# Second-layer queries: a product split in two levels, a key bias sum moved to ScalarE, and where the work around them stands

## The chip, the cores and the metric

The kernel runs on one NeuronCore of a Trainium2 chip. The metric is the device time of one execution in microseconds (us), lower is better. In what follows TensorE is PE in the profile, VectorE is DVE, ScalarE is ACT, GpSimd is POOL, and SyncE, which only issues loads and stores here, is SP.

## The reference

Two cross-attention layers are applied to x (8 batches of 100 rows and 1024 columns), each against the same context (8 x 1444 x 512), all in float32:

```
layer 0:  Q = x Wq + bq, K = ctx Wk + bk, V = ctx Wv + bv
          x <- x + (softmax over keys(Q K^T / 32) V) Wo + bo
layer 1:  q = x Wq + bq, k = ctx Wk + bk, v = ctx Wv + bv
          w = softmax over the QUERIES (axis 1) of q k^T / 32
          x <- layernorm(w v + x) * gamma + beta
```

The output is x. In layer 1 the softmax runs over the 100 query rows of one batch, for each of the 1444 keys.

## The kernel before, in words

**Algebra.** Scores are not made from keys. The kernel first multiplies the two weight matrices of a layer, Wq Wk^T (a product called qk, 1024 x 512), and uses x (Wq Wk^T) as queries of width 512, called g0T and g1T, against the raw context. In the same way Wv Wo of layer 0 becomes one matrix, vo. What the biases add to the scores is a vector for each batch, the key bias (`c`), made from `kb`, the sum over the 8 chunks of x of chunk times a column of weights.

**Strassen-like products.** Most products are made with seven half-size products for eight (`weight_products`, `queries`, `project0`, `project1`); a line like `left_sums` makes the four sums S1 to S4 of the left operand, T1 to T4 are those of the right. The seven results are called x, z, y, x, w, x, y by the PSUM bank that they go to, and VectorE adds them to their blocks. `inner_product` does the same once more inside one of the seven, with names like g_z_x, vo_w_y, o_q_x: the z, w or q product of the outer seven, in seven again. Seven with 1/8 less work each level, for extra sums on VectorE. In `queries(1, ...)`, the queries of layer 1, the products z (4 matmuls become 7 of half the width, and so on) and w are split a second time; the last one, y with S4 and B22, is not.

**Order.** The order of PE is the program's own. The steps are generators (`yield`, `next`, `run`, `islice`) that are advanced by hand, so that the matmuls of two stages alternate. The order of the other engines is a scheduler's, except where `vector.in_order` or `keep_in_program_order` pins an instruction. [...]

**Stages in time** (of the profiled execution): qk of layer 0 (4 to 52 us), vo (52 to 100), queries of layer 0 (100 to 137), qk of layer 1 (137 to 184), attention of layer 0, where the scores of batch b + 2 (`s`, line 923) alternate with the weighted context rows of batch b (`A`, line 894) (184 to 351), the projection `project0` (o_..., to 381), the queries of layer 1 (g_..., 381 to 413), attention of layer 1 (413 to 605, with `project1` and the finishing of rows between) and the last batch.

**The places that the change touches.**

- Line 107: eight matmuls on a tile of ones at the start, while the first weights load. A matmul in float32 stands as two records in the trace.
- `weight_products` for vo0 (lines 490 to 510): VectorE makes T2, then the second half of a scaled sum (`accs[...][1]()`, four operations of 1024 columns on a prob tile), adds the two z banks, and makes S2 in place of S1 (tile vo_s). The product `product(X, S2, T2, False)` follows, named vo_x.
- `project0`, its last part: W is the inner w product (o_w_x, o_w_z, o_w_y, ...) whose first step is run, then the o_x banks are added to x (`add(1, 0, 1, X_)`), then the rest of W is run.
- `queries`: S4 is made in the place of A12, after g_y. Steps that `yield` let the caller put other work between.
- `key_bias_sums("kb1", ...)`: eight VectorE operations (one `tensor_scalar`, seven `scalar_tensor_tensor` of 800 columns, tile kb) spread over the steps of the queries. Layer 0's kb0 is already made in another way, by `scaled_sum`: ScalarE scales each chunk into a tile of its own, and transfers that add (`transfer_added`, on POOL's queue, line 567) sum them in pairs.
- The first scores of layer 1, `scores(0)` (16 matmuls s of 361 columns), then the last step of the queries (product y, g_y), then the scores of batch 1. The key bias c is made two matmuls before the end of the scores of batch 0 and read by ScalarE, which moves the scores to the tile prob. Then VectorE makes 16 transposes (w<-prob), three maxima (negmax), ScalarE the exponentials, VectorE the reciprocal and the product that ends w. PE's first A matmul of batch 0 reads w.
- `LATER` tells for (layer, batch) how many steps of that softmax are made at once with the scores; the others are left to the caller. The softmax of batch 0 is not in it, so all of it is put out right after the scores and ahead of g_y's adds.
- Buffers: `unit` is a pool of 10 (weights, context rows c, transposed context cT, rooms of sums); `bank` a pool of 6 PSUM banks and `bank2` one of 2; `row` and `weight_rows` pools of 3.

Of the kernel before, what the change touches and what calls it, by code (L numbers as in the profile page):

```python
# [27 lines left out]
ALU = mybir.AluOpType  # L28
# [4 lines left out]
B, T, E = 8, 100, 1024  # L33
# [13 lines left out]
G = 4  # L47
GT = G * T
SETS = (range(0, 4), range(4, 7), range(7, 8))
LATER = {(1, 5): 0, (1, 7): 16}  # L50
SCALE = 1.0 / math.sqrt(E)
EPS = 1e-6

# [2 lines left out]
def two_layer_cross_attention(ctx: ExitStack, tc: tile.TileContext, a: dict, out: bass.AP):  # L56
# [11 lines left out]
    def bank(name):  # L68
        return psum.tile([P, 512], F32, tag="ps", name=name)

    def bank2(name):
        return psum2.tile([P, 512], F32, tag="ps2", name=name)
# [31 lines left out]
    ones = const.tile([P, P], F32, tag="ones", name="ones")  # L104
    nc.vector.memset(ones, 1.0)
    warm = bank("warm")
    for _ in range(8):
        nc.tensor.matmul(warm[:, :P], ones, ones, start=True, stop=True)
    ident = const.tile([P, P], F32, tag="ident", name="ident")
    make_identity(nc, ident)  # L110
# [29 lines left out]
    def run(*parts):  # L140

        parts = list(parts)
        while parts:
            parts = [g for g in parts if next(g, parts) is not parts]
# [35 lines left out]
    def combine(to, x, y, op, engine=vector):  # L180
        for t, p, q in zip(to, x, y):
            engine.tensor_tensor(t, p, q, op)
# [69 lines left out]
        add(0, 1, Y)  # L252
        yield

    def inner_product(name, lhs, rhs, nb, width, t, put, add, right=None, left=None, ahead=False, spare=bank2):

        h, w = nb // 2, width // 2
        m = len(singles(lhs)) // 2

        def quarters(x, n):
            if len(x) == 1:
                return ([x[0][:, m * k : m * k + m, c]] for c in halves(n) for k in range(2))
            return ([x[m * k + i][:, c] for i in range(m)] for c in halves(n) for k in range(2))

        def room(x, t):
            t = t.rearrange("p (i n) -> p i n", i=m)  # L270
            return [t] if len(x) == 1 else [t[:, i, :] for i in range(m)]

        A11, A12, A21, A22 = quarters(lhs, nb * P)
        B11, B21, B12, B22 = quarters(rhs, width)
        lw, rw = m * h * P, 0 if right else m * w
        S1, T1 = room(lhs, t[:, :lw]), right or room(rhs, t[:, lw : lw + rw])

        S2, S3, S4, T2, T3, T4 = A11, A21, A12, B11, B12, B21
        if ahead:

            S2, S4 = (room(lhs, t[:, o : o + lw]) for o in (lw + rw, 2 * lw + rw))
            if not right:
                T2, T4 = (room(rhs, t[:, o : o + rw]) for o in (3 * lw + rw, 3 * lw + 2 * rw))
        if right:
            T1, T2, T3, T4 = right

        if left:
            S1, S2, S3, S4 = left

        def second():  # L290
            combine(T2, B22, T1, ALU.subtract)
            combine(S2, S1, A11, ALU.subtract)

        def fourth():
            combine(T4, B21, T2, ALU.subtract)
            combine(S4, A12, S2, ALU.subtract)

        combine(S1, A21, A22, ALU.add)
        combine(T1, B12, B11, ALU.subtract)
        combine(S3, A11, A21, ALU.subtract)  # L300
        combine(T3, B22, B12, ALU.subtract)
        if ahead:
            second()
            fourth()

        def product(ps, left, right, fresh):
            half_product([ps], left, right, fresh, h, w)

        def steps():
            X = bank(f"{name}_x")  # L310
            product(X, A11, B11, True)
            put(0, 0, X)
            if not ahead:
                second()
            yield
            Z = spare(f"{name}_z")
            product(Z, A12, B21, True)
            add(0, 0, Z)
            if not ahead:
                fourth()  # L320
            yield
            Y = bank(f"{name}_y")
            product(Y, S1, T1, True)
            put(1, 1, Y)
            yield
            product(X, S2, T2, False)
            put(0, 1, X)
            yield
            W = spare(f"{name}_w")
            product(W, A22, T4, True)  # L330
            put(1, 0, W)
            yield
            product(Y, S4, B22, False)
            add(0, 1, Y)
            yield
            product(X, S3, T3, False)
            add(1, 1, X)
            add(1, 0, X)
            yield

        return steps()
# [5 lines left out]
    def weight_products(name, left, right, l_width, r_width, scaled, between=None):  # L347
# [91 lines left out]
        def add(r, c, banks):  # L439
            for j in range(2):  # L440
                to = block(r, c, j)
                vector.tensor_tensor(to, to, banks[j].rearrange("p (n w) -> p n w", n=per), ALU.add)
# [53 lines left out]
        if name != "qk0":  # L496
            T2, T4 = B11, B21
            combine(T2, B22, T1, ALU.subtract)
            if name == "vo0":
                accs[scaled[0][0]][1]()  # L500
            add(0, 0, Z)
        combine(S1, S1, A11, ALU.subtract)
        S2 = S1
        if name != "vo0":
            combine(A21, A11, A21, ALU.subtract)
        if name != "qk0":
# [146 lines left out]
    def queries(layer, w, u, between=None):  # L653
# [17 lines left out]
        def add(r, g, banks):  # L671
            for j in range(2):
                to = dst[g][:, 2 * r + j, :]
                vector.tensor_tensor(to, to, banks[j][:, :GT], ALU.add)
# [13 lines left out]
            return put, add  # L688

        def pair(n):  # L690

            return [(bank2 if layer and n == "y" else bank)(f"g{layer}_{n}{j}") for j in range(2)]

        def product(banks, lhs, rhs, fresh):
            half_product(banks, lhs, rhs, fresh, nb, GT)
# [1 line left out]
        t = None  # L697

        def inner(n, lhs, rhs, put, add, right=None, at=0, left=None):
            spare = bank if layer else bank2  # L700
            return inner_product(f"g{layer}_{n}", lhs, rhs, nb, GT, t[:, at:], put, add, right, left, spare=spare)

        def four(t):

# [2 lines left out]
        def steps():  # L707
            nonlocal t
            S3, S4 = A21, A12
            if layer:  # L710
                combine(S1, A21, A22, ALU.add)
                yield
                combine(S2, S1, A11, ALU.subtract)
                yield
                combine(S3, A11, A21, ALU.subtract)
                yield
            T1, T2 = ([wide(f"g{layer}_t{n}")] for n in (1, 2))
            if layer:
# [29 lines left out]
            if layer:  # L748

                vector.in_order = False  # L750
                yield
                vector.in_order = True
                S4 = A11
                combine(S4, A12, S2, ALU.subtract)
                _, more = parts(0, 0)
                Z = inner("z", A12, B21, more, more, four(T3[0]))
                combine(T2, B22, T1, ALU.subtract)
                run(Z)
                combine(T3, B22, B12, ALU.subtract)
            else:  # L760
                combine(S4, A12, S2, ALU.subtract)
# [7 lines left out]
            V = half_steps(X, S3, T3, False, nb, GT)  # L769
            for n, _ in enumerate(inner("w", A22, T1, *parts(1, 0))):  # L770
                next(V)
                if layer:
                    yield
                if layer == 0 and n == 1:
                    between()
                elif layer == 0 and n == 3:

                    add(0, 1, Y)
                    _, more = parts(0, 1)
                    Q = inner("q", S4, B22, more, more, four(T2[0]), E)  # L780
            if layer == 0:
                next(Q)
                run(V)
                yield
                run(islice(Q, 4))
                add(1, 0, X)
                add(1, 1, X)
                run(Q)
                vector.in_order = False
            else:  # L790
                run(V)
                add(1, 0, X)
                add(1, 1, X)
                vector.in_order = False
                yield
                product(Y, S4, B22, False)
                add(0, 1, Y)
            yield

        return dst, steps()  # L800
# [212 lines left out]
    def project0(AS, A0):  # L1013
# [10 lines left out]
        def pair(n, bank=bank):  # L1024
            return [bank(f"o0_{n}{j}") for j in range(2)]
# [4 lines left out]
        def add(j, r, g, banks):  # L1030
            e = 4 * j + 2 * r
            add_to_queries([e, e + 1], g * GT, GT, banks)
# [22 lines left out]
        product(X_, A_[0], B11, True)  # L1055
        combine(T2, B22, T1, ALU.subtract)
        add(1, 0, 0, X_)
        Y = pair("y")
        product(Y, S[0], T1, True)
        combine(T4, B21, T2, ALU.subtract)  # L1060
# [18 lines left out]
        add(1, 1, 1, Y)  # L1079
        product(X_, S_[1], T2, False)  # L1080

        next(W)
        add(1, 0, 1, X_)
        run(W)
        add(1, 0, 1, Y)
# [212 lines left out]
            vector.in_order = False  # L1298
    next(o0)
    next(queries1)  # L1300
    run(o0)

    kb1, more = key_bias_sums("kb1", wqbk1)
    steps = queries1
    for n, _ in enumerate(islice(steps, 5 + 7)):
        if n > 2:
            vector.in_order = True
            next(more, None)
    run(more)
    biases1 = key_biases("c1", kb1, bqbk1)  # L1310
    next(biases1)
    vector.in_order = False
# [12 lines left out]
    run(islice(scores1, LC * NB - 2))  # L1325
    key_bias[1] = next(biases1)
    run(scores1)
    run(steps)
    run(first_scores(1, 1, softmax1))

    finished = {(4, 2): 0, (4, 16): 1, (4, 30): 2, (5, 34): 3, (7, 2): 4, (7, 15): 5, (7, 28): 6}
# [43 lines left out]
```

## Time and profile before

| | us |
|---|---|
| median of 3 runs | 635.04 (634.66 to 635.53) |
| the profiled execution's own time | 634.84 |
| its span, first to last instruction | 632.9 |
| PE busy | 621.5 |
| DVE busy | 487.1 |
| ACT busy | 163.9 |
| POOL busy | 102.2 |
| DMA, mean rate | 218 GB/s |

The profile is one execution. A row of a timeline gives the start, the time from the first to the last of the records merged in it, the engine, the line, the operation, what is written and read, the shape, and in brackets the idle time before it and what ended that. A row of the waits gives the total, the number and the longest. Matmuls are pipelined: the ends shown for PE are modelled and reach past the next start, so the step from start to start is the better measure of a product.

### The profile page before, as it was taken

The numbers are of one execution on the slowest core, as the hardware profiler recorded it, in microseconds if no ns is written. First come the engines' busy times: TensorE is split into PE (matmuls) and PEld (weight loads), VectorE is DVE, ScalarE is ACT, GpSimd is POOL, SyncE is SP. The second block draws the span as 40 slices with busy tenths as digits, with TensorE's granted clock in tenths as the row PEclk, the third lists the DMA queues.
The fourth block names the chain that finished last, engine by engine and source line by source line (L and its number), as shares of the span: only waits on it lengthen the run. The fifth ranks groups of instructions, "written<-read, shape, count | busy, mean of one in ns | idle before, by whom it ended". The sixth has DMA issues, their size and how long they took to land.

```text
span 632.9 us, 10570 instructions
## 1 busy us (share of the span) xinstructions
PE 621.5 (98%) x4142; PEld 534.2 (84%) x4142; DVE 487.1 (77%) x995; ACT 163.9 (26%) x380; POOL 102.2 (16%) x133
## 2 busy tenths in 40 slices
PE   9999999999999999999999999999999999999994
PEld 8886467688985999999989666756999999999992
DVE  2987979996885797666758687968777659898886
ACT  1322012324304234423230001113433240325301
POOL 2110101112230000000000001008111220544054
PEclk9999999999999999999999999999999999999998
DMA  8969848335999788988942308255888990599002
GB/s 272 293 136 348 274 140 272 68 81 111 203 315 382 283 311 299 327 307 306 312 155 88 101 0 325 96 194 192 295 305 307 316 324 2 201 330 332 27 22 84
DMA packets 52521, 138.27 MB, mean 218 GB/s; under 512 B 4403, under 2 KB 8755, under 8 KB 52471
## 3 DMA queue, kind: packets, MB, share of 16 engines
q1 hardware_dynamic: 46792, 120.85, 55.1%
q0 software_dynamic: 5280, 16.26, 11.7%
q8 instruction: 33, 0.54, 0.3%
q10 hardware_dynamic: 398, 0.47, 0.2%
q14 instruction: 18, 0.14, 0.1%
HBM read 123.36 MB, written 3.28 MB: 200 GB/s over the span
## 4 chain that ended last, share of the span: by engine, by line
PE 90%; DMA 3%; DVE 3%; issue 1%; POOL 1%; ACT 0%; POOLq 0%; DVEq 0%; SPq 0%
PE s L923 25%; PE A L894 25%; PE qk_x L163 6%; PE o_x L163 5%; PE g_x L163 4%; DMA vo<-in_L_xattn_Wo 3%; PE o_y L163 3%; PE g_y L163 3%; PE vo_x L163 2%; PE qk_y L163 2%; PE qk_z L163 2%; DVE vo L96 1%; PE o_z L163 1%; PE o_w L163 1%; PE qk_w L163 1%
## 5 line engine op out<-in xcount | busy, mean ns | idle before, releaser
L894 PE MATMUL A<-w,c 120*128 120x100 f32 (+1 forms) x1536 | 249.6, 265 | 0.0
L894 PEld LDWEIGHTS A<-w,c 120*128 120x128 f32 (+1 forms) x1536 | 218.0, 190 | 2.8
L96 DVE STREAM_TRANSPOSE w<-prob 32x384 f32<-32x384 f32 (+1 forms) x256 | 143.7, 561 | 27.6 <-ACT prob L962 9.7
L923 PE MATMUL s<-cT,g1T 128*100 128x131 f32 (+2 forms) x592 | 122.8, 296 | 0.0
L923 PE MATMUL s<-cT,g0T 128*100 128x131 f32 (+2 forms) x592 | 122.7, 296 | 0.0
L923 PEld LDWEIGHTS s<-cT,g1T 128*100 128x100 f32 x592 | 78.4, 167 | 8.6 <-issue 0.3
L923 PEld LDWEIGHTS s<-cT,g0T 128*100 128x100 f32 x592 | 78.2, 167 | 8.4 <-PE c L593 0.4
L935 ACT ACTIVATE prob<-s,c 100x393 f32<-100x393 f32 (+2 forms) x64 | 34.5, 560 | 112.7 <-PE s L923 99.5
L1111 ACT ACTIVATE w<-w,negmax 120x100 f32<-120x100 f32 (+1 forms) x96 | 34.8, 364 | 82.7 <-DVE negmax L96 82.7
L955 DVE TENSOR_REDUCE maxima<-prob 100x1 f32<-100x394 f32 (+3 forms) x32 | 16.5, 528 | 23.4 <-ACT prob L935 23.1
L1321 POOL DMA_DIRECT2D wv<-in_L_xattn_Wv x1 | 0.8, 772 | 191.2 <-PE o_x L163 191.2
L163 PE MATMUL qk_x<-qk 128*128 128x256 f32 x128 | 29.7, 380 | 0.0
L1130 POOL TENSOR_TENSOR part<-w 120x500 f32<-120x500 f32 x8 | 10.9, 1368 | 112.9 <-DVE rstd L1205 28.6
L163 PEld LDWEIGHTS qk_x<-qk 128*128 128x128 f32 x128 | 23.3, 190 | 3.0 <-ACT qk L437 0.2
L669 ACT ACTIVATE g1T<-g_x,k 128x400 f32<-128x400 f32 x4 | 2.4, 594 | 69.2 <-PE g_x L163 69.0
L1111 ACT ACTIVATION_READ_ACCUMULATOR w<-w,negmax 120x1 f32 (+1 forms) x96 | 17.9, 187 | 0.0
L1210 POOL TENSOR_TENSOR z<-z,vectors 100x1024 f32<-100x1024 f32 x7 | 16.5, 2356 | 8.2 <-ACT z L1209 8.2
L96 DVE TENSOR_TENSOR xT<-xT,o_x 128x400 f32<-128x400 f32 (+1 forms) x32 | 15.8, 539 | 2.2 <-PE o_x L163 2.0
L1188 PE MATMUL z<-ident,xT 128*100 128x128 f32 x64 | 16.3, 273 | 0.0
L1209 ACT ACTIVATE z<-z,rstd 100x1024 f32<-100x1024 f32 x7 | 8.0, 1149 | 31.9 <-POOL rstd L1206 31.9
L1192 DVE SCALAR_TENSOR_TENSOR z<-vectors,r,z 100x512 f32<-100x512 f32 x16 | 11.8, 740 | 4.8 <-PE z L1188 4.8
L163 PE MATMUL vo_x<-vo 128*128 128x512 f32 x32 | 15.3, 595 | 0.0
(415 smaller groups left out, 987.8 us busy)
## 6 DMA issues: line engine op xcount, KB each, us to landing
cT<-in_ctxT SPq DMA_DIRECT2D x64, 722.0 KB, 6.3
c<-in_ctx SPq DMA_DIRECT2D x48, 768.0 KB, 8.3
c<-in_ctx SPq DMA_DIRECT2D x16, 512.0 KB, 5.9
vo<-in_L_xattn_Wo SPq DMA_DIRECT2D x8, 512.0 KB, 10.1
qk<-in_L_xattn_WqT SPq DMA_DIRECT2D x8, 512.0 KB
qk<-in_L_xattn_WqT SPq DMA_DIRECT2D x15, 256.0 KB, 5.8
c<-in_ctx SPq DMA_DIRECT2D x16, 224.0 KB, 5.9
xT<-in_xT SPq DMA_DIRECT2D x2, 1600.0 KB
```

The costliest lines, as they stand in the source:

```text
L96: ins = getattr(nc.vector, op)(*args, **kw)
L163: nc.tensor.matmul(banks[n // per][:, n % per * width : (n % per + 1) * width], lhs[i][:, n * P : (n + 1) * P], rhs[i], start=(fresh and i ...
L894: nc.tensor.matmul(ps[:, k * T : (k + 1) * T], c[m // CQ][:r, m % CQ, k * P : (k + 1) * P], w[:r, m, :], start=(m == 0 and k == 0), stop=( ...
L923: nc.tensor.matmul(banks[n // per][:T, cuts[n] - o : cuts[n + 1] - o], q[:, k, t0 : t0 + T], cT[k][:, cuts[n] : cuts[n + 1]], start=(k == ...
L935: nc.scalar.activation(p[:, part], ps[:T, : part.stop - part.start], AF.Identity, bias=key_bias[layer][:T, b : b + 1], scale=SCALE,)
L955: nc.vector.tensor_reduce(maxima[:, n : n + 1], p[:, part], AX.X, ALU.max)
L1111: nc.scalar.activation(w[:r, m0 + m, :], w[:r, m0 + m, :], AF.Exp, bias=negmax[:r, m : m + 1], accum_out=total[:r, m : m + 1])
L1130: add(part, w[:MR, 0:5, :], w[:MR, 5:10, :], ALU.add)
L1188: nc.tensor.transpose(ps[:T, e * P : (e + 1) * P], xT[:, 4 * j + e, b * T : (b + 1) * T], ident)
L1192: nc.vector.scalar_tensor_tensor(z[:, half], bv1[j][:T], s["r"], ps[:T, :], ALU.mult, ALU.add)
L1209: nc.scalar.activation(z, z, AF.Copy, scale=rstd)
L1210: nc.gpsimd.tensor_tensor(z, z, beta[:T], ALU.add)
```

## The change

Seven edits; the last three are small moves:

1. The last product of layer 1's queries (y with S4 and B22) is made by `inner_product` (q), seven products of 200 columns for eight matmuls of 400. It stands at the same place of PE's order, after the scores of batch 0. The banks that the inner z and w products use change to make room for it (the `spare` argument goes; y goes to `bank`).
2. S4 of layer 1's queries gets a buffer of its own (one more `unit`) and is made before the first product; `project0` gets one more `yield`, so that this step comes between its parts.
3. `kb1` is made like kb0: ScalarE scales seven chunks into seven tiles, six adding transfers sum them, a seventh adds the sum to VectorE's one chunk.
4. The softmax of batch 0 (`LATER[(1, 0)] = 0`) is put out along the steps of the split product: three transposes after each of its last three yields, the rest behind it.
5. Six matmuls for eight at the start.
6. In vo0, S2 is made before the second half of the scaled sum and the adding of z.
7. In `project0`, four steps of W for one are run before the o_x banks are added.

Stores, outputs and all other products stay. In PE's order nothing else changes. On DVE the sequence between the key bias and the first maximum of batch 0 becomes: the add of q_x, T2, S2, the add of q_z, T4, S4, the adds of q_y and q_x, 3 transposes, the add of q_w, 3 transposes, the add of q_y, 3 transposes, two adds of q_x, 7 transposes. On ACT one of the four prob<-s moves of batch 1 comes to stand ahead of the exponentials of batch 0. On POOL's queue the seven adding transfers stand among the loads of wv, gamma, beta and bv: three, wv, gamma, one, beta, bv, one, bv, two.

```
-LATER = {(1, 5): 0, (1, 7): 16}
+LATER = {(1, 0): 0, (1, 5): 0, (1, 7): 16}
...
-    for _ in range(8):
+    for _ in range(6):
         nc.tensor.matmul(warm[:, :P], ones, ones, start=True, stop=True)
...
             combine(T2, B22, T1, ALU.subtract)
-            if name == "vo0":
-                accs[scaled[0][0]][1]()
-            add(0, 0, Z)
+            if name != "vo0":
+                add(0, 0, Z)
         combine(S1, S1, A11, ALU.subtract)
         S2 = S1
+        if name == "vo0":
+            accs[scaled[0][0]][1]()
+            add(0, 0, Z)
...
         def pair(n):
-            return [(bank2 if layer and n == "y" else bank)(f"g{layer}_{n}{j}") for j in range(2)]
+            return [bank(f"g{layer}_{n}{j}") for j in range(2)]
...
                 combine(S3, A11, A21, ALU.subtract)
+                yield
+            if layer:
+                S4 = [unit(f"g{layer}_s4")[:, :E].rearrange("p (c l) -> p c l", c=H)]
+                combine(S4, A12, S2, ALU.subtract)
                 yield
...
-                S4 = A11
-                combine(S4, A12, S2, ALU.subtract)
...
             for n, _ in enumerate(inner("w", A22, T1, *parts(1, 0))):
                 next(V)
-                if layer:
-                    yield
                 if layer == 0 and n == 1:
                     between()
-                elif layer == 0 and n == 3:
+                elif n == 3:
                     add(0, 1, Y)
                     _, more = parts(0, 1)
                     Q = inner("q", S4, B22, more, more, four(T2[0]), E)
...
                 vector.in_order = False
                 yield
-                product(Y, S4, B22, False)
-                add(0, 1, Y)
+                vector.in_order = True
+                for _ in Q:
+                    yield
+            vector.in_order = False
...
         add(1, 0, 0, X_)
+        yield
         Y = pair("y")
...
-        next(W)
+        run(islice(W, 4))
         add(1, 0, 1, X_)
         run(W)
...
     next(o0)
     next(queries1)
+    next(o0)
+    next(queries1)
     run(o0)
-    kb1, more = key_bias_sums("kb1", wqbk1)
+    tiles = [t[:, : B * T] for t in prob] + [weight_rows(f"kb1_{n}")[:, : B * T] for n in range(3)]
+    kb1, more = key_bias_sums("kb1", wqbk1, tiles + [row("kb1_6")[:, : B * T]])
+    run(more)
     steps = queries1
-    for n, _ in enumerate(islice(steps, 5 + 7)):
-        if n > 2:
-            vector.in_order = True
-            next(more, None)
-    run(more)
+    run(islice(steps, 5))
+    vector.in_order = True
     biases1 = key_biases("c1", kb1, bqbk1)
...
     key_bias[1] = next(biases1)
     run(scores1)
-    run(steps)
+    softmax = batches[0]["softmax"]
+    for n, _ in enumerate(steps):
+        run(islice(softmax, 3 if n > 2 else 0))
+    run(softmax)
     run(first_scores(1, 1, softmax1))
```

More of the change, by code (lines that the diff above doesn't have):

```diff
@@ L253, in seven_products, with inner_product @@
         yield
-    def inner_product(name, lhs, rhs, nb, width, t, put, add, right=None, left=None, ahead=False, spare=bank2):
+    def inner_product(name, lhs, rhs, nb, width, t, put, add, right=None, left=None, ahead=False):
         h, w = nb // 2, width // 2
@@ L315, in steps @@
             yield
-            Z = spare(f"{name}_z")
+            Z = bank2(f"{name}_z")
             product(Z, A12, B21, True)
@@ L328, in steps @@
             yield
-            W = spare(f"{name}_w")
+            W = bank2(f"{name}_w")
             product(W, A22, T4, True)
@@ L699, in inner @@
         def inner(n, lhs, rhs, put, add, right=None, at=0, left=None):
-            spare = bank if layer else bank2
-            return inner_product(f"g{layer}_{n}", lhs, rhs, nb, GT, t[:, at:], put, add, right, left, spare=spare)
+            return inner_product(f"g{layer}_{n}", lhs, rhs, nb, GT, t[:, at:], put, add, right, left)
         def four(t):
@@ L788, in steps @@
                 run(Q)
-                vector.in_order = False
             else:
```

## The prediction

> **What bounds the kernel now.** I read the page's busy times first, then the waits of TensorE (PE), then the timeline of each engine around the places that the change touches.
>
> ```profile
> PE 621.5 (98%) x4142; PEld 534.2 (84%) x4142; DVE 487.1 (77%) x995; ACT 163.9 (26%) x380; POOL 102.2 (16%) x133
> ```
>
> PE is busy 98% of 632.9 us, so a gain can only be PE work taken out or one of PE's few idle gaps closed. The waits of PE name all of those gaps but the tail:
>
> ```profile
> PE warm L108 <- DVE ones L105: 1.1, 1, 1.1
> PE vo_x L163 <- DVE vo_s L96: 1.0, 1, 1.0
> PE o_w_y L163 <- DVE xT L96: 0.6, 1, 0.6
> PE g_z_x L163 <- DVE g_t L96: 0.4, 1, 0.4
> ```
>
> The change aims at the second and third and at the matmuls of the last query product. Around that product there is a place with little room, in the timelines of PE, VectorE (DVE) and ScalarE (ACT):
>
> ```profile
> 422.61 5.54 PE L163 MATMUL g_y<-xT,qk 128*128 128x400 f32 x16
> 427.98 9.89 PE L923 MATMUL s<-cT,g1T 128*100 128x361 f32 x32
> 437.71 0.36 PE L894 MATMUL A<-w,c 120*128 120x100 f32 x2
> ```
> ```profile
> 421.99 0.23 DVE L650 TENSOR_SCALAR c<-c,bqbk 128x8 f32<-128x8 f32 x1
> 424.26 9.46 DVE L96 STREAM_TRANSPOSE w<-prob 32x384 f32<-32x384 f32 x16 [2.05 <-ACT prob L935]
> 433.75 0.57 DVE L96 TENSOR_TENSOR g1T<-g1T,g_y 128x400 f32<-128x400 f32 x1
> 434.24 1.51 DVE L96 TENSOR_REDUCE negmax<-w 120x4 f32<-120x400 f32 x3
> ...
> 436.63 0.66 DVE L96 TENSOR_TENSOR w<-w,rtotal 120x400 f32<-120x400 f32 x1
> ```
>
> PE needs the first group of softmax weights w of batch 0 at 437.71; DVE delivers it at 436.63 + 0.66 = 437.29. No wait of PE shows, but the margin is 0.4 us, and DVE is packed from 424.26 on: 16 transposes at 0.59, an add, the maximum at 434.24, then 3.05 us through ACT's exponentials to w.
>
> [...]the 16 warm records take 3.50 us (0.219 each for 128 columns), the next 8, of 256 columns, take 1.89 us: the same time for twice the columns. [...]what the change puts ahead of the transposes delays them in full. The trace shows the strictness: at 373.73 two o_x adds stand ahead of a finished o_w_z.
>
> **The change part by part**, in the clock of this profile.
>
> *Warm-up, 8 to 6 matmuls* (16 to 12 records). They end at 1.06 + 12 x 0.21 = 3.6 instead of 4.4. The first loads were issued at 0.74 and land 3.2 us later at the earliest, 3.9; so qk_x starts near 3.95 instead of 4.40, part of it still at half clock: **-0.36**. At most -0.45[...]. Nothing takes it back: the four chunks of T4 end between 15.8 and 19.1 and qk_w uses one every 1.73 from 18.2; most loads of vo wait for PE's own releases; and the last Wo lands at 63.4, 0.9 ahead of its use by vo_z at 64.3.
>
> *vo: S2 ahead of the scaled sum.*
>
> ```profile
> 66.13 7.03 PE L163 MATMUL vo_y<-vo_s 128*128 128x512 f32 x16
> 74.20 7.10 PE L163 MATMUL vo_x<-vo,vo_s 128*128 128x512 f32 x16 [1.04 <-DVE vo_s L96]
> ```
>
> vo_x waits for vo_s, made at 73.63 behind four sums of 1024 columns (67.82 to 72.5) and two vo_z adds (72.44 to 73.7). After the change the four vo_s (1.43) come at 67.8 and end at 69.3; vo_y ends at 73.1 and vo_x follows at once: **-1.1** (idle 1.04 plus start-up). The sums and adds then end where vo_s ended, and T4 keeps its time of 77.4 against a need at 80.1. On to 98 DVE has 2.2 and 1.0 us idle, so it follows. Both ends: -1.0 to -1.2.
>
> *o0: four steps of W ahead of the two o_x adds.* The second o_w_y waits at 374.7 for the first one's add, which stands behind two o_x adds of 0.5. In the new order w_x, w_z, w_y, w_x are added by 374.8 and that wait goes. Late next: the o_x adds end at 375.85 and the third o_x product wants its second bank at 375.67, 0.2 lost. o_x began at 376.15; seven products at 0.336 from 372.91 end at 375.3: 0.8 less 0.2 = **-0.6** (0.3 to 0.8).
>
> *S4 made sooner*, in a buffer of its own. One DVE operation (1.22) moves from 386.9 to 355.1, ahead of T4 and T3 of project0. T4 ends at 357.3 for o_w at 359.48, T3 at 358.2 for o_x at 362.16, and DVE's idle 0.91 and 1.44 there take it up: **0**. Without those gaps, +1.2 at most. At 386.9 DVE was waiting for PE anyway: no gain there. The buffer comes from the stream pool: loads of batch 2 (one c block, one cT block) now wait for the split product, until about 425 and 427.5, instead of 420 and 422.8. With 6 to 8 us to landing they come by 436, for use after 442: **0**.
>
> *Key bias sum.* DVE loses seven of eight operations (0.63 + 7 x 0.96, about 6.7), but PE waited for none of them: **0** directly. ACT gains seven of about 1 us; it is idle from before 386, and four can run from 373, when xT's first half is final. The other three end at about 387, delaying g1T<-g_x from 386.2 to 387, needed at 397. On POOL's queue seven adding transfers of 400 KB interleave with wv, gamma, beta and bv. In the trace such a transfer took 4.0 to 4.8 alone, wv and the vectors 11 to 13 together. First three 375 to 385; kb_1<-kb_2 behind wv until about 391; then three in a row at 4.8: about 406. VectorE reads it at 415: room of 9 us, **0**. wv slips by about 3 us to 393 and is not used before its sums on POOL, which now start when PE leaves qk at 412.
>
> *The last product.* Out: 16 records g_y, 5.37. In: 7 products of 4 records of 200 columns, 0.675 each, 4.73. Its closest row is g_z, the same seven in a row on the same engines: 392.06 to 397.20 is 5.14, since its fourth product waits for DVE's S2. I take 5.14: **-0.23** of PE; ends 0 and -0.64. s then ends at 437.5.
>
> *What stands ahead of the transposes.* The eight VectorE operations that the split product puts there (add, T2, S2, add, T4, S4, add, add) have g_z's rows as their pattern:
>
> ```profile
> 393.01 0.36 DVE L96 TENSOR_TENSOR g1T<-g1T,g_z_x 128x200 f32<-128x200 f32 x1 [1.52 <-PE g_z_x L163]
> 393.29 0.57 DVE L96 TENSOR_TENSOR g_t<-xT,g_t 128x400 f32<-128x400 f32 x1
> 393.78 0.42 DVE L96 TENSOR_TENSOR qk<-g_t,qk 128x256 f32<-128x256 f32 x1
> ...
> 395.21 0.35 DVE L96 TENSOR_TENSOR g1T<-g1T,g_z_y 128x200 f32<-128x200 f32 x1
> 395.48 0.35 DVE L96 TENSOR_TENSOR g1T<-g1T,g_z_x 128x200 f32<-128x200 f32 x1
> ```
>
> The first add comes 0.95 after the product's start (392.06); the last starts at 395.48 and frees DVE 0.28 later, 3.7 after the start. From 422.6 that is 426.3. The transposes start at 426.3 instead of 424.26. Between them are put q_w, q_y and two q_x adds (4 x 0.28), and one g_y add (0.49) goes from ahead of the maximum. The maximum starts at 426.3 + 9.46 + 1.12 = 436.9 instead of 434.24; + 3.05 gives w at 440.0. ACT puts one prob<-s of batch 1 ahead of the exponentials, done by 436.3, so no later. PE is ready at 437.5 and waits 2.5: A begins at 440.0 instead of 437.71: **+2.3** (1.7 to 2.8), with the -0.23 in it. Behind the waiting matmul all of PE queues. Nothing takes this back: A of batch 1 has its w at 453.6 for 457.5 and both move together.
>
> *Sum*: -0.36 - 1.1 - 0.6 + 2.3 = **+0.25**. On the profiled execution's own 634.84 (span 632.9 and 1.9 around it) that is 635.1; its time lies 0.2 below the median 635.04, so 635.3.
>
> **Rivals.**
>
> *No wait at A.* If the split product's VectorE work found room in the 2.05 us that DVE is idle at 422.2, w would come as before and all gains stay: 635.04 - 2.06 - 0.23 = **632.8**. For it: that idle time exists. Against: the operations end 2 us after it, since each waits for a product of 0.675, and four adds come later.
>
> *The key bias is late* (slower; times in this profile's clock, in which all of the stage moves together). PE's c product at 421.4 needs two DVE operations of 1.2 after the last adding transfer. It decides from a landing at about 418.9. If POOL's last four transfers take 9 us each (as beside wv) instead of 4.8, from 387 they land at 423: 4 us of wait ahead of everything counted, **639.4**. Against: only wv and the vectors run beside them, and those land by 394.
>
> [...]
>
> *The split saves nothing*: with two levels PE has 14 x 200 columns for 8 x 400, an eighth less; as g_z shows, waits can eat it. That is in the forecast already: DVE ends last, not PE.
>
> **How the numbers follow.** About 0.2% (1.27 us) is what a measurement of this kernel can tell from no change. Forecast (gains of about 2 against a wait of about 2.3): 0.68, own range 634.3 to 636.3 (each part at its ends, some up and some down). No wait at A or a much shorter one: 0.15. Late bias 0.05, slow window 0.06, another wait of over 1 us that I don't see 0.06: 0.17. So faster 0.15, same 0.68, slower 0.17, and the likeliest case is no change. Leaving out some 0.1 on each side, the range is 634.0 to 636.8.
>
> **What would show it.** Right: PE's waits lose vo_x and o_w_y and gain one of about 2.5 at A <- DVE w between 437 and 440; DVE's first maximum of batch 0 14.3 after the last product starts (11.6 before); qk_x from about 3.95; c without a wait. Wrong: no wait at A, or c waiting for c_sums, or the first 8 us at half clock.

## The result, and the profile after

| | before | after |
|---|---|---|
| median | 635.34 (634.66 to 637.44, 5 runs) | 637.83 (637.67 to 638.36, 5 runs) |
| profiled execution, own time | 634.84 | 637.67 |
| its span | 632.9 | 635.9 |
| PE busy | 621.5 | 622.2 |

The ratio is 1.0046, with a 95% interval of 1.0034 to 1.0059: slower by 2.5 us by these medians, by some 2.9 by the ratio, where no change (635.3) was forecast. All times are in microseconds.

Read the waits of PE first. Of the changed kernel (total, number, longest):

```profile
PE A L895 <- ACT w L1113: 2.7, 1, 2.7
PE vo_q_x L163 <- DVE vo L96: 1.1, 1, 1.1
PE warm L108 <- DVE ones L105: 1.1, 1, 1.1
PE g_z_x L163 <- DVE g_t L96: 0.3, 1, 0.3
PE vo_w_x L163 <- DVE vo L96: 0.2, 1, 0.2
```

The waits of vo_x and o_w_y are gone, and the one at A has come, all as forecast. But vo_q_x and vo_w_x are new, and no step of the prediction has them.

The timeline of DVE around S2 of vo (the changed kernel) tells where they come from:

```profile
68.45 0.43 DVE L96 TENSOR_TENSOR vo_s<-vo_s,vo 128x256 f32<-128x256 f32 x1 [1.09 <-PE vo_y L163]
70.17 0.43 DVE L96 TENSOR_TENSOR vo_s<-vo_s,vo 128x256 f32<-128x256 f32 x1 [1.29 <-PE vo_y L163]
71.89 0.43 DVE L96 TENSOR_TENSOR vo_s<-vo_s,vo 128x256 f32<-128x256 f32 x1 [1.29 <-PE vo_y L163]
73.60 0.43 DVE L96 TENSOR_TENSOR vo_s<-vo_s,vo 128x256 f32<-128x256 f32 x1 [1.29 <-PE vo_y L163]
73.95 0.75 DVE L96 TENSOR_SCALAR prob<-vo,L_xattn_bv 128x1024 f32<-128x1024 f32 x1
...
79.77 2.49 DVE L96 TENSOR_TENSOR vo<-vo,vo 128x512 f32<-128x512 f32 x4
```

S2 is written over S1 (`combine(S1, S1, A11, ...)`, tile vo_s), and vo_y, running from 66.54, still reads S1. Each of the four operations waits for vo_y to leave its chunk, 1.72 apart. DVE stands idle for 1.09 + 3 x 1.29 = 4.96 with the scaled sum queued behind it. In the old order that sum filled just this time (the kernel before):

```profile
67.82 0.74 DVE L96 TENSOR_SCALAR prob<-vo,L_xattn_bv 128x1024 f32<-128x1024 f32 x1
68.60 3.92 DVE L96 SCALAR_TENSOR_TENSOR prob<-vo,L_xattn_bv,prob 128x1024 f32<-128x1024 f32 x3
...
73.63 1.43 DVE L96 TENSOR_TENSOR vo_s<-vo_s,vo 128x256 f32<-128x256 f32 x4
```

In the changed kernel T4 ends at 79.77 + 2.49 = 82.3, where the prediction kept 77.4.

The PE timeline of the changed kernel then shows both sides, the gain and what it costs:

```profile
66.54 7.03 PE L163 MATMUL vo_y<-vo_s 128*128 128x512 f32 x16
73.40 7.03 PE L163 MATMUL vo_x<-vo,vo_s 128*128 128x512 f32 x16
80.60 1.21 PE L163 MATMUL vo_w_x<-vo 128*128 128x256 f32 x4 [0.16 <-DVE vo L96]
...
97.57 1.13 PE L163 MATMUL vo_q_x<-vo 128*128 128x256 f32 x4 [1.13 <-DVE vo L96]
```

vo_x follows vo_y 6.86 later, as forecast (8.07 before). But vo_w_x needs T4, and DVE stays late up to the vo_q sums: from vo_w_x to the first g_x PE takes 20.88 instead of 19.09. The whole stretch from vo_z to g_x takes 101.48 - 59.67 = 41.81 instead of 40.96.

The place of the split product, first PE with the waiting A, then DVE:

```profile
423.04 0.84 PE L163 MATMUL g_q_x<-xT,g_s 128*128 128x200 f32 x4
...
428.11 9.90 PE L924 MATMUL s<-cT,g1T 128*100 128x361 f32 x32
440.72 0.43 PE L895 MATMUL A<-w,c 120*128 120x100 f32 x2 [2.71 <-ACT w L1113]
```
```profile
422.42 0.83 DVE L652 TENSOR_SCALAR c<-c,bqbk 128x8 f32<-128x8 f32 x1
423.92 0.36 DVE L96 TENSOR_TENSOR g1T<-g1T,g_q_x 128x200 f32<-128x200 f32 x1 [0.67 <-PE g_q_x L163]
...
426.39 0.35 DVE L96 TENSOR_TENSOR g1T<-g1T,g_q_x 128x200 f32<-128x200 f32 x1
426.77 1.74 DVE L96 STREAM_TRANSPOSE w<-prob 32x384 f32<-32x384 f32 x3
...
437.59 1.52 DVE L96 TENSOR_REDUCE negmax<-w 120x4 f32<-120x400 f32 x3
...
440.05 0.58 DVE L96 TENSOR_TENSOR w<-w,rtotal 120x400 f32<-120x400 f32 x1
```

The product takes 428.11 - 423.04 = 5.07 (before 5.37). The eight operations (add, T2, S2, add, T4, S4, add, add) occupy DVE until 426.7, the first maximum comes 14.55 after the product's start (before 11.63), and w is done at 440.6. A begins 17.68 after the product's start, against 15.10. The waits list names ACT for it, which is writing the next group of w at that moment. But A begins 0.09 after the end of DVE's product (440.63), and in d and g below 0.11 and 0.10 after it, so the wait is for DVE, as forecast; the time was lost ahead of that product, by the late transposes.

The span's 3.0 is put together from marks on PE (starts of products) in the two profiles:

| stretch | before | after | difference | forecast |
|---|---|---|---|---|
| start to vo_z | 59.27 | 59.67 | +0.40 | -0.36 |
| vo_z to g_x | 40.96 | 41.81 | +0.85 | -1.1 |
| o_w_x to o_q_x | 5.93 | 5.29 | -0.64 | -0.6 |
| last product of queries to A | 15.10 | 17.68 | +2.58 | +2.3 |
| all the rest | | | -0.2 | 0 |

### The profile page after: what moved, and what is told of

It reads as the page before. It is cut to its first block, busy times and chain, and to the rows that moved or that the text cites. A ratio compares the mean times of both kernels' runs of the same rounds, so it can differ in the third digit from the quotient of the medians.

```text
span 635.9 us, 10627 instructions
## 1 busy us (share of the span) xinstructions
PE 622.2 (98%) x4150; PEld 535.4 (84%) x4150; DVE 485.7 (76%) x1004; ACT 170.2 (27%) x387; POOL 108.1 (17%) x140
## 4 chain that ended last, share of the span: by engine, by line
PE 90%; DVE 7%; issue 1%; POOL 1%; ACT 0%; POOLq 0%; DVEq 0%; ACTq 0%
PE A L895 24%; PE s L924 24%; PE qk_x L163 7%; PE o_x L163 5%; PE g_x L163 4%; DVE vo L96 3%; PE o_y L163 3%; PE qk_z L163 2%; PE qk_y L163 2%; PE g_y L163 2%; PE o_z L163 1%; PE o_w L163 1%; PE vo_x L163 1%; PE qk_w L163 1%; PE vo_y L163 1%
## 5 line engine op out<-in xcount | busy, mean ns | idle before, releaser
L569 POOL DMA_DIRECT2D prob<-prob x8 | 6.9, 856 | 209.3 <-PE o_y L163 184.5
L960 ACT ACTIVATE prob<-prob,negmax 100x1444 f32<-100x1444 f32 x8 | 12.0, 1498 | 11.2 <-DVE negmax L958 11.2
```

The lines of the kernel that those rows point to most:

```text
L960: nc.scalar.activation(p, p, AF.Exp, bias=negmax, accum_out=total)
```

## The experiments

Two groups of four kernels; those of a group ran on one chip beside the kernel before (medians 635.08 in the first group, 634.95 in the second). Each ratio is to that. PE marks of all of them:

| kernel | ratio, interval | median | clock full at | vo_z | vo_z to g_x | product to A |
|---|---|---|---|---|---|---|
| a_warm8 | 1.0057 [1.0036, 1.0077] | 639.25 | 4.60 | 59.49 | 41.80 | 17.67 |
| b_vo_back | 1.0046 [1.0032, 1.0061] | 638.24 | 6.71 | 60.34 | 39.69 | 17.68 |
| c_s2_elsewhere | 1.0032 [1.0021, 1.0044] | 637.22 | 6.74 | 60.27 | 39.69 | 17.68 |
| d_no_split | 1.0010 [1.0000, 1.0019] | 635.59 | 5.41 | 59.68 | 41.79 | 15.34 |
| e_three_moves | 0.9968 [0.9956, 0.9979] | 633.28 | 6.61 | 60.26 | 39.69 | 15.10 |
| f_two_moves | 0.9972 [0.9960, 0.9984] | 633.56 | 6.61 | 60.48 | 39.69 | 15.10 |
| h_nosplit_s2 | 0.9983 [0.9973, 0.9993] | 633.99 | 4.27 | 59.52 | 39.70 | 15.34 |
| g_split_room | 0.9984 [0.9977, 0.9992] | 634.00 | 6.15 | 59.98 | 39.69 | 15.36 |

"Clock full at" is when the trace of the profiled execution has PE's clock turn from half to full: 4.13 before, 5.52 after. In the profile after, the qk_x records (256 columns each) follow one another at 0.43 ahead of it and at 0.22 behind it; in the one before, the warm records (128 columns) at 0.21 and 0.11. This is called the turn below; a drop is a later return to half clock, which the tables of stretches show as a granted clock of 0.50.

**a_warm8.** The theory under test: six warm-up matmuls make the clock turn late.

```
-    for _ in range(6):
+    for _ in range(8):
         nc.tensor.matmul(warm[:, :P], ones, ones, start=True, stop=True)
```

> The changed kernel (637.8) with eight warm-up matmuls again. Theory (the shorter warm-up with its 0.3 us gap lets the clock turn full one step later: 5.52 us for 4.13): the turn comes back to about 4.1 us, the mean clock to 0.997, and the time falls by 0.8 to 637.0. Rival (the turn comes at a random phase, whatever the warm-up): mean clock between 0.995 and 0.997 from run to run, median within 0.3 of 637.8.

639.25: slower, not faster. The turn at 4.60 did come earlier than in the profile after, and vo_z only 0.18 earlier, so this kernel alone doesn't decide the theory; e and f below do. Something else shows, in the table of stretches of this kernel (time, then busy time and number of instructions of PE, PEld, DVE, ACT, POOL, then the granted clock, DMA share, GB/s):

```profile
434.70:438.10 3.40, 3.11 (x11) 1.41 (x9) 3.29 (x7) 0.62 (x2) 0.00 (x0) 1.00 0.90 259
438.10:441.51 3.41, 0.99 (x9) 1.02 (x10) 1.96 (x6) 3.41 (x19) 0.00 (x0) 1.00 1.03 336
441.51:444.92 3.41, 3.41 (x19) 3.41 (x19) 2.13 (x5) 2.32 (x9) 1.47 (x3) 0.50 0.11 46
444.92:448.30 3.38, 3.38 (x34) 3.38 (x33) 3.25 (x7) 0.00 (x0) 2.13 (x5) 1.00 0.12 8
```

The wait at A lies almost wholly within one 3.41 stretch, PE is busy 0.99 of it, and the next stretch runs at half clock: 19 matmul records in it, 34 in the one after. At half the rate that should cost an estimated 3.41 / 2 = 1.7 on top of the wait, and it does: from A to the end this profile takes 196.87, the profile after 195.18. Three of the five executions (639.25 to 639.65) have a mean clock of 0.994, the other two (638.20 and 638.27) of 0.995 and 0.996, which fits a drop in three of them. In the profile after, no drop follows the same wait. Stretches of the same length, laid out from its own turn at 5.52, divide the wait in two, with PE busy 2.45 and 1.66:

```profile
435.56:438.97 3.41, 2.45 (x9) 1.02 (x7) 3.32 (x7) 1.29 (x5) 0.00 (x0) 1.00 0.90 292
438.97:442.38 3.41, 1.66 (x15) 1.69 (x16) 1.65 (x5) 3.41 (x21) 0.00 (x0) 1.00 0.86 265
442.38:445.80 3.42, 3.42 (x35) 3.42 (x34) 2.42 (x5) 1.65 (x5) 2.07 (x4) 1.00 0.05 19
```

**b_vo_back.** The changed kernel with vo in the old order:

```
             combine(T2, B22, T1, ALU.subtract)
-            if name != "vo0":
-                add(0, 0, Z)
+            if name == "vo0":
+                accs[scaled[0][0]][1]()
+            add(0, 0, Z)
         combine(S1, S1, A11, ALU.subtract)
         S2 = S1
-        if name == "vo0":
-            accs[scaled[0][0]][1]()
-            add(0, 0, Z)
```

> The changed kernel with the order of before in vo0 (sums and z adds ahead of S2). Theory (S2 written over S1 has to wait for vo_y, chunk by chunk, so DVE stands idle 5 us and T4 ends at 82 for 77.4): the waits vo_w_x and vo_q_x go, vo_x <- vo_s of 1.0 comes back, PE loses 0.7 less between vo_z and the queries of layer 0: 637.1. Rival (the loss there comes from loads that fell otherwise): the wait at vo_q_x stays at 1 us and the time at 637.8.

The new waits in vo are gone: 39.69 from vo_z to g_x, 2.12 less than after. The time did not follow (638.24). In the profile the late turn (6.71) takes 0.67 back at vo_z, and the drop behind the wait at A, at 440.20 to 443.62, takes 1.58 more. Of the other executions only the mean clock is known (0.991 to 0.996). The wait of 1.0 at vo_x, which was expected to return, did not:

```profile
67.20 7.03 PE L163 MATMUL vo_y<-vo_s 128*128 128x512 f32 x16
74.07 7.03 PE L163 MATMUL vo_x<-vo,vo_s 128*128 128x512 f32 x16
```
```profile
73.33 1.42 DVE L96 TENSOR_TENSOR vo_s<-vo_s,vo 128x256 f32<-128x256 f32 x4
```

This says something about the kernel before. PE came 1.07 later to vo_z, but S2 came no later (73.33, before 73.63): ahead of it DVE waits for loads of WvT and Wo in both profiles, until 60.20 and 63.16 here, 60.49 and 63.46 before. So the wait of 1.04 in the profile before is what an early PE finds; when PE is late, S2 is there already.

**c_s2_elsewhere.** The new order, but S2 gets the place of A11, which vo_y doesn't read:

```
-        combine(S1, S1, A11, ALU.subtract)
-        S2 = S1
+        S2 = A11 if name == "vo0" else S1
+        combine(S2, S1, A11, ALU.subtract)
```

> The changed kernel with S2 of vo0 written over A11, which PE has read long before, for over S1. Theory (the write over an operand in use is the whole trouble): DVE makes S2 at once near 67.5, no DVE idle before it, vo_x follows vo_y, T4 ends near 77, the waits vo_w_x and vo_q_x go: 1.8 less than 637.8, 636.0, and 1.1 less than the kernel with the order of before there. Rival (the sums behind it are late anyway): only the 0.7 comes back, 637.1.

637.22, ratio 1.0032. The waits of PE in this kernel:

```profile
PE A L895 <- ACT w L1113: 2.7, 1, 2.7
PE warm L108 <- DVE ones L105: 1.1, 1, 1.1
PE g_z_x L163 <- DVE g_t L96: 0.4, 1, 0.4
```

Neither vo_x nor vo_w_x nor vo_q_x waits. So it was the place of S2 that made the new order lose. That the new order gains over the old one isn't shown here: b, with nearly the same turn, takes the same 39.69, and the two intervals overlap (medians 638.24 and 637.22). This profile too has one stretch at half clock behind the wait at A (440.23 to 443.64, after a stretch with PE busy 0.92 of 3.41), which is why it gains less in time than in vo and misses the 636.0 expected.

**d_no_split.** The changed kernel with the last product whole, the banks as before, and the softmax of batch 0 at once:

```
-LATER = {(1, 0): 0, (1, 5): 0, (1, 7): 16}
+LATER = {(1, 5): 0, (1, 7): 16}
...
-                vector.in_order = True
-                for _ in Q:
-                    yield
+                product(Y, S4, B22, False)
+                add(0, 1, Y)
...
```

> The changed kernel with the last query product whole again and the softmax of batch 0 put out at once; S4 early, key bias by ScalarE and the three small moves stay. Theory (VectorE's work of the split product ahead of and among the transposes is what A waits for): no wait of PE at the first A of layer 1; from the start of the last product to that A 15.1 us for 17.7: 2.6 less, 635.2. Rival (the key bias by ScalarE and transfers makes c or prob late): a wait at A or c of over 1 us stays and the time is above 636.5.

635.59, 2.2 below the changed kernel's median: the split and its order on DVE cost 17.68 - 15.34 = 2.34 in the trace. No wait at A is left, but A stands 0.24 later than before, and DVE and POOL tell why:

```profile
422.46 0.83 DVE L652 TENSOR_SCALAR c<-c,bqbk 128x8 f32<-128x8 f32 x1
```
```profile
420.78 2.48 POOL L182 TENSOR_TENSOR wv_s<-wv,wv_s 128x512 f32<-128x512 f32 x2
```

The operation on c took 0.23 before and takes 0.83 here. With S4 made sooner the buffer of qk comes free at the last g_x, so that POOL's sums of wv begin at 413 (428 before) and run beside it. It is 0.83 in after, c and d, in which they do, and in h; it is 0.23 in before, e and g, in which they come later. In after, c and d it ends 0.02 to 0.03 after the last of these sums (423.29 and 423.26 here). What makes it 0.60 longer beside them was not shown: no run here took POOL's sums alone away.

**e_three_moves.** The kernel before with only the three small moves, S2 written over A11:

```
-    for _ in range(8):
+    for _ in range(6):
...
-            if name == "vo0":
-                accs[scaled[0][0]][1]()
-            add(0, 0, Z)
-        combine(S1, S1, A11, ALU.subtract)
-        S2 = S1
+            if name != "vo0":
+                add(0, 0, Z)
+        S2 = A11 if name == "vo0" else S1
+        combine(S2, S1, A11, ALU.subtract)
+        if name == "vo0":
+            accs[scaled[0][0]][1]()
+            add(0, 0, Z)
...
-        next(W)
+        run(islice(W, 4))
```

> The kernel before with the three small moves only (six warm-ups, S2 of vo0 ahead of the scaled sum but written over A11 in place of S1, four steps of W ahead of the o_x adds); last product whole, key bias sum on VectorE, S4 in the old place. Theory (the vo move was spoilt only by S2 being written over the S1 that vo_y still reads): vo_z to g_x takes 39.7 to 40.0, waits vo_w_x and vo_q_x are absent, o0 gains 0.64, the start about 0.3; 633.4 to 634.6, ratio to before 0.998. Rival (S2 ahead of the sums is bad wherever it is written, because the sums then reach T4 late): a wait of about 1 at vo_q_x stays and the time is 635.3 or more.

633.28, ratio 0.9968: faster than both kernels. DVE around S2 now reads:

```profile
67.54 1.43 DVE L96 TENSOR_TENSOR vo<-vo_s,vo 128x256 f32<-128x256 f32 x4
68.88 0.75 DVE L96 TENSOR_SCALAR prob<-vo,L_xattn_bv 128x1024 f32<-128x1024 f32 x1
...
74.70 2.49 DVE L96 TENSOR_TENSOR vo<-vo,vo 128x512 f32<-128x512 f32 x4
```

This is the row that the prediction had in mind: four S2 in 1.43, the sums at once behind them, T4 done at 77.2. Against the profile before, vo_z to g_x takes 1.27 less and o_w_x to o_q_x 0.64 less, while the later turn takes 0.99 back at vo_z. One profile can't divide the 1.7 between the medians in this way.

**f_two_moves.** The same with the old eight warm-ups.

> As e_three_moves but with the old eight warm-ups. Theory (the clock turns full at a time of its own[...], so two warm-ups fewer are worth their 0.3 on the average): 0.1 to 0.5 slower than e_three_moves, 633.7 to 635. Rival (six warm-ups make the clock turn later by about 1.4, as between the profiles of before and after): 0.4 or more faster than e_three_moves.

633.56, 0.28 above e_three_moves; the intervals overlap, so the time alone decides nothing. The profiles do: in both the clock turned at 6.61, and vo_z stands at 60.26 with six and 60.48 with eight. In this pair two matmuls fewer are worth 0.22, and there is no sign that they move the turn.

**h_nosplit_s2.** d_no_split with the edit of c_s2_elsewhere.

> The changed kernel with the last product whole and its softmax at once (as d_no_split), and S2 of vo0 over A11 (as c_s2_elsewhere): S4 sooner and the key bias sum on ScalarE stay. Theory: 0.9 to 1.1 faster than d_no_split (635.6), so about 634.6, as vo_q_x's wait of 1.1 goes; and 0.2 slower than e_three_moves, since POOL's sums start at 412 and the operation on c beside them takes 0.83 for 0.23, so A begins 15.3 after the start of g_y, not 15.1. Rival (the S2 place is worth nothing, c_s2_elsewhere was faster by chance): 635.4 or more.

633.99, ratio 0.9983 where d_no_split had 1.0010: some 1.7 for the place of S2 alone, and the two intervals don't meet. Against e_three_moves it is 0.7 slower, not the 0.2 expected; the intervals overlap, the traces differ by the 0.24 at A and, the other way, by an earlier clock turn, and the rest stays open. This profile does show the order's gain: with a turn at 4.27, nearly that of before (4.13), vo_z to g_x takes 39.70 instead of 40.96.

**g_split_room.** The split product with DVE's work made beforehand or put behind (S2 of vo0 over A11, and S4 of the queries back in its old place, are not shown):

```
+    def late(add):
...
+            if len(seen) in (1, 3, 4):
+                add(*args)
+            else:
+                later.append(lambda: add(*args))
...
-                    Q = inner("q", S4, B22, more, more, four(T2[0]), E)
+                    Q = inner("q", S4, B22, more, more, four(T2[0]), E) if layer == 0 else inner_product(
+                        "g1_q", S4, B22, nb, GT, t[:, 768:], late(more), late(more), four(T2[0]), ahead=True
+                    )
...
-        run(islice(softmax, 3 if n > 2 else 0))
+        run(islice(softmax, (0, 1, 1, 14, 0, 0, 0, 0)[n]))
+    vector.in_order = True
+    for n in (2, 1, 1, 1):
+        next(softmax, None)
+        for _ in range(n):
+            later.pop(0)()
     run(softmax)
...
```

> The changed kernel with S2 of vo0 over A11, S4 in its old place over A11 of the queries, and the split product's VectorE work out of the way: its second and fourth sums are made ahead, before g_w_y's add, in rooms of their own; of its eight adds only three (x, y, second x) stand ahead of or among the transposes, five come behind the first maxima. Theory (the wait at A is nothing but VectorE's order): the wait of 2.7 at A goes to 0.5 or less, A begins 14.7 to 15.0 after the start of the last product (before 15.1, after 17.7), and the time is 0 to 0.4 below e_three_moves, about 633.7. The chain from c through 16 transposes to w still takes some 14.7, so PE's saved 0.64 can't all show. Rival (seven small products cost PE their gain themselves, or lack banks): new waits of 0.3 or more inside g_q, A later than 15.3, time 635 or more.

634.00, where about 633.7 was expected. Its waits of PE, but for the warm-up's:

```profile
PE A L909 <- issue: 0.7, 1, 0.7
PE g_z_x L163 <- DVE g_t L96: 0.4, 1, 0.4
PE s L938 <- ACT prob L950: 0.4, 1, 0.4
```

The seven products now run without a gap, 426.09 - 421.36 = 4.73, so the waits inside g_q that the rival wanted aren't there. The wait at A falls from 2.7 to 0.7: the bulk of it was DVE's order. But A comes 15.36 after the start, not 14.7 to 15.0. Behind it a scores matmul waits 0.4 for ACT, whose next prob<-s stands behind the exponentials, and A to the end takes 195.91 (195.22 in e_three_moves): this 0.7 is lost again. The timeline of DVE shows what is late:

```profile
420.73 0.23 DVE L652 TENSOR_SCALAR c<-c,bqbk 128x8 f32<-128x8 f32 x1
...
433.27 1.52 DVE L96 TENSOR_REDUCE negmax<-w 120x4 f32<-120x400 f32 x3
...
435.74 0.88 DVE L96 TENSOR_TENSOR w<-w,rtotal 120x400 f32<-120x400 f32 x1
```

From the end of c (420.96) to w (436.62) is 15.66; in e_three_moves it is 436.40 - 421.31 = 15.09. One add stands ahead of the transposes and two, 0.4 each with the gaps around them, among them, for one of 0.5 behind them; and the product that ends w took 0.88 beside POOL's sums (0.68 in e_three_moves, beside them too, 0.57 in d, where they were over). PE would have been ready at 436.0. So the split frees 0.64 of PE in a place where the chain from c to w ends only 0.4 ahead of A (436.40 and 436.81 in e_three_moves): with nothing put into that chain, it could have gained 0.4 at the most, by this estimate.

## Why the prediction was wrong

**Failed: vo, S2 ahead of the scaled sum (-1.1; measured +0.85).** The sentence that fails is "the four vo_s (1.43) come at 67.8 and end at 69.3". It counted their durations and the queue of DVE, and not whom they overwrite. vo_s is S1, vo_y reads S1 to its end at about 73.5, and the fourth started at 73.60. The step looked only at what S2 needs, and its cover "the sums and adds then end where vo_s ended" went with it: the sums began at 73.95, not at the forecast 69.3. e shows DVE's row as forecast once S2 is written over A11; in c, e and h vo_z to g_x then takes 39.69 to 39.70.

**A smaller slip in the same step**: the wait of 1.04 was taken as a constant of the kernel. It was what was left over in an execution with the clock turn at 4.13; with the turn at 6.71 (b_vo_back) it is nil. The move, rightly made, is thus worth 1.26 with an early turn (39.70 in h against 40.96 before) and nothing with a late one (39.69 in c, new order, and in b, old order).

**Mis-sized: warm-up (-0.36; +0.40 in the profile, -0.22 by e against f).** That qk_x starts at 3.94 was right (forecast 3.95), though not in every execution: in h it starts at 4.17, behind a wait of 0.2 for a load. What the profile lost is the turn at 5.52 for 4.13: 1.39 more at half clock costs an estimated 1.39 / 2 = 0.70, and without it vo_z would be 0.30 earlier, not 0.40 later. The turn lay between 4.13 and 6.74 in the ten profiles, at 4.13 to 6.61 with eight warm-ups and at 4.27 to 6.74 with six. The forecast compared with the one turn that the profile before had.

**Mis-sized: the wait at A (+2.3; measured +2.58).** The transposes started 3.73 after the product (forecast 3.7) and the first maximum came 14.55 after it (forecast 14.3). The difference lies among the transposes, between which four adds stand in three places: 437.59 - 426.77 is 10.82, where the forecast added 9.46 + 1.12 = 10.58. An add takes 0.38 to 0.39 from its start to the next transpose there, where the forecast counted 0.28: the gaps at each change are not in a sum of durations.

**Right**: o0 (-0.64 for -0.6, the wait of o_w_y gone), the last product (5.07 for 5.14), S4 and the key bias sum at about 0 in the changed kernel: c doesn't wait, so *the key bias is late* falls. (Their side effect, the slower operation on c, shows only without the split, as 0.24 in d and h.) The 0.06 given to a slow window was the author's estimate, with no trace behind its size. 1.95 of the 2.8 that the forecast missed lies in vo, and e and f, with and without the 0.3 of idle time behind the warm-up, turn at the same 6.61. *No wait at A* falls by its 2.7. *The split saves nothing* is right in effect, as the forecast had it: PE's product is 0.30 shorter, and DVE ends last.

With the vo step at +0.85, the A step at +2.58, o0 at -0.64 and the start at +0.40, the sum is +3.2; the spans differ by 3.0.

## What to carry to other kernels

When an operation is moved ahead on an engine, ask first which readers its destination still has: here each of four in-place sums waited 1.09 to 1.29 for the product that read the old contents, and the scaled sum queued behind them waited too, with DVE idle for 4.96. Given another place, the same move lost nothing (39.69 in c and in b), and gained 1.26 where PE was early (h). A wait seen in one profile may be the remainder of a start-up that differs from run to run: 1.04 with the turn at 4.13, none with it at 6.71. And work taken out of one engine gains only as much as the next chain that this engine waits for is ahead at that place: of the 0.64 freed in g, an estimated 0.4 at the most.

## What the hardware showed that was not expected

- Behind a single wait of PE of 2.7 the clock dropped to half for the next 3.41 in a, b and c; PE had been busy for 0.99, 0.82 and 0.92 of the 3.41 ahead of the drop. In after, with the same wait, it did not drop; of the stretches laid out there, the one with the least work had PE busy for 1.66. What decides it was not shown: no run moved the wait alone.
- From the turn at the start to the drop it was 441.51 - 4.60 = 436.91 in a_warm8, 440.20 - 6.71 = 433.49 in b_vo_back and 440.23 - 6.74 = 433.49 in c_s2_elsewhere: two alike, and one 3.42 longer, about the length of one drop (3.41).
- A DVE operation of 0.23 on 128 x 8 values took 0.83 beside POOL's sums, and ended 0.02 to 0.03 after the last of them.
